# Two attention layers on one core: softmax shares turned by VectorE and spread by DMA, and the second pass in another order

## The chip, the core and the metric

The kernel runs on one core of one Trainium2 chip. A core has a matrix engine (TensorE, PE in the profile), a vector engine (VectorE, DVE), an activation engine (ScalarE, ACT), a general engine (GpSimd, POOL) and a queue engine (SyncE, SP) that issues most of the DMAs. Sixteen DMA engines move the data. On-chip data lie in SBUF (128 partitions); TensorE writes to PSUM, from which VectorE and ScalarE read. Each engine works through its own instructions strictly in order and waits on semaphores, so a late operand holds everything that is queued behind the waiting instruction on that engine.

The metric is the device time of one execution in microseconds (us). Before the change the median of four runs is 3569.33 us, from 3559.91 to 3572.44.

## What is computed

Two layers on 8 images of 32 x 32 places with 512 channels, all in fp32. The first is group norm, a projection to queries, keys and values, attention with 8 heads of 64 channels over all 1024 places, and an output projection that is added to the input:

```
qkv    = groupnorm(x) @ w_qkv + b_qkv
weight = softmax(q k^T / 64)              # 1024 x 1024 per head and image
x      = x + (weight @ v) @ w_out + b_out
```

The second is deformable attention. The first layer's result is layer-normed; a strided 7x7 depthwise convolution of its query projection gives 256 sampled places per image; keys and values come from these; then attention of all 1024 places over the 256 samples, an output projection and a small MLP:

```
att   = softmax(q k^T) @ v                # 1024 x 256 per head and image
z     = att @ mo_w + mo_b + x
out   = gelu(layernorm(z) @ mlp_w + mlp_b) + z
```

In both layers the softmax is split: scores minus their row maximum go through the exponential, whose row sums are gathered on the way, and the product with the values is divided by the sums only at the end. "Shares" are these reciprocals of the sums.

## The kernel before, in words

Work is cut in units. Each handles one pair of heads (two heads of 64 channels fill 128 partitions) and some query rows. The two passes keep one list of steps, `due`: `at(place, step)` (L348) files a step at a place counted in units, and `run_due` (L351) runs all steps below a place in order of place. An order wrapper (`InOrder`, L43) keeps each engine's instructions in the order of the program, so the places fix the order on every engine. What runs is: L387 to L799 the first pass, L802 to L1244 the second.

**First pass** (L387). A unit is 128 query rows of one image and one pair of heads against 1024 keys: 8 images x 4 pairs x 8 = 256 units. `MovedAttention.push` (L189) makes the scores (`scores`, L91: matmul into the PSUM tiles `sc`, row maxima `nmax` on VectorE, exponentials `e` with their sums on ScalarE), turns them in blocks of 32 x 32 on VectorE (`sq`), and after each second unit `moved` (L205) issues 16 DMAs that finish the transposition (`et<-sq`). Three units later `part` (L216) multiplies `et` with the values into `av`, of which PSUM holds one buffer. Four units make a block of 512 rows; at its end the shares are applied. In between, the `due` list holds the next projections, norms, the previous image's output projection, and depthwise convolution taps for the second layer.

**Second pass** (L802). A unit is 512 query rows and one pair of heads against 256 keys: 8 images x 2 halves x 4 pairs = 64 units. `unit_steps` (L1136) files, for unit n: scores at n, `moved` for each head at n + 0.12 and n + 0.14 (turn by VectorE, store to memory `sq_d<-sq`, load back `et<-sq_d`), shares at n + 0.2, their turn at n + 0.62, the product with the values at n + 1.15 and the scaling at n + 1.155; the next unit's query projection at n + 0.17. `back_steps` (L1060) files the output side, one tile of 128 rows per unit: `joined` (output projection `mm<-wo,attH`, sum `z` and its statistics) at n + 0.05, `norm` (`zn`) at n + 0.13, `turned` (transposition `mm<-ident,zn`, copies `zT`) at n + 0.6, `mlp` (`mm<-wm,zT`, the last projection) at n + 0.72, `biased` at n + 0.95, and for two tiles together `gelu` and `end`. `rstd` inside `joined` needs one small POOL instruction (`mv<-mv,minus_half`), for which `norm` waits. `conv_steps` (L1164) adds convolution taps in two lanes: lane 0 on VectorE (`chunk<-pad,dww,chunk`), lane 1 on ScalarE (`parts`) with the additions on POOL (`chunk<-parts,chunk`); `point_steps` (L1189) adds the sampling of the next image.

**The shares**, in both passes (L157 to L178). The sums lie with query rows on partitions, the product `av` has channels on partitions and query rows along the free dimension, so the shares must be turned. `share` takes the reciprocal on VectorE and copies each value 64 times (`rep`, 128x512); `turn` has TensorE transpose `rep` in four 128x128 pieces (`mm<-ident,rep`) and ScalarE copy the result to `inv`; `scale` multiplies `av` by `inv` on VectorE. This happens once in each block of the first pass (64) and once in each unit of the second (64).

## Time and profile before

| | |
|---|---|
| median of four runs | 3569.33 us |
| the profiled execution | 3555.69 us |
| its span on the core | 3554.0 us |
| PE busy | 3438.4 us (97%) |
| DVE busy | 2550.3 us (72%) |
| ACT busy | 1894.3 us (53%) |
| POOL busy | 1560.0 us (44%) |
| first pass | from the start to about 2220 us |
| preparation of the second pass | about 2220 to 2308 us |
| second pass, 64 units | 2308.71 us to the end |
| granted clock of TensorE | 0.992 in the mean |

The page gives busy time of each engine over the span. A share of busy time is an average over stages with different limits, so the windows (busy time of each engine in chosen stretches) are read beside it. The list of waits tells, for each engine, which other engine's result ended its idle time. The timeline lists instructions in order of time: start, duration, engine, operation, output <- inputs, shapes, count, and in brackets the idle time before it and what ended it. Matmuls are pipelined, so the starts of neighbours tell more than the durations. Almost all instructions carry line L54, that of the order wrapper; they are told apart by their tiles.

### The profile page before, as it was taken

How to read it: one execution, taken by the hardware profiler on the slowest of the kernel's cores; microseconds unless marked ns; L12 is line 12 of the kernel's file. 1: busy time of each engine (PE TensorE's matmuls, PEld its weight loads, DVE VectorE, ACT ScalarE, POOL GpSimd, SP SyncE). 2: the span in 40 equal slices, each digit the busy share in tenths (PEclk: the TensorE clock that was granted, in tenths of full speed). 3: DMA queues.
4: the chain of work that ended last, by engine and by line, in shares of the span. 5: the costliest groups of instructions: out<-in, count | busy, mean ns of one | idle time of the engine just before them, and what ended most of it. 6: DMA issues, size and time to landing. Idle time of an engine off the chain costs nothing.

```text
span 3554.0 us, 45846 instructions
## 1 busy us (share of the span) xinstructions
PE 3438.4 (97%) x15080; PEld 1712.3 (48%) x15080; DVE 2550.3 (72%) x3373; ACT 1894.3 (53%) x4061; POOL 1560.0 (44%) x1899
## 2 busy tenths in 40 slices
PE   7999999999999999999999998889999999999998
PEld 3554554554554554455455454534444444444443
DVE  4767778888888888888888786166778577564554
ACT  2443356576566566566567562245556465644442
POOL 1002226646646646655655654214445354531222
PEclk9999999999999999999999999999999999999999
DMA  4656666656656656666656667444545454454543
GB/s 141 162 152 170 181 160 188 195 148 177 206 157 176 197 158 174 193 165 184 192 166 163 190 169 206 126 153 159 195 156 188 148 183 167 162 204 159 189 142 118
DMA packets 358525, 606.01 MB, mean 171 GB/s; under 512 B 54576, under 2 KB 152880, under 8 KB 356240
## 3 DMA queue, kind: packets, MB, share of 16 engines
q1 hardware_dynamic: 327648, 500.99, 47.5%
q0 software_dynamic: 29488, 100.00, 9.1%
q8 instruction: 120, 1.97, 0.2%
q10 hardware_dynamic: 1152, 2.10, 0.2%
q14 instruction: 117, 0.96, 0.1%
HBM read 212.83 MB, written 121.63 MB: 94 GB/s over the span
## 4 chain that ended last, share of the span: by engine, by line
PE 82%; DVE 5%; ACT 4%; POOL 3%; DMA 3%; issue 2%; SPq 1%; ACTq 0%; POOLq 0%; DVEq 0%
PE mm L54 52%; PE sc L54 16%; PE av L54 14%; ACT e L54 2%; DVE sq L54 2%; SPq L54 1%; DMA et<-sq_d 1%; DVE nmax L54 1%; POOL chunk L54 1%; DMA et<-sq 1%; DMA sq_d<-sq 1%; DVE stats L54 1%; POOL res L54 0%; DVE zn L54 0%; ACT L54 0%
## 5 line engine op out<-in xcount | busy, mean ns | idle before, releaser
L54 ACT ACTIVATE e<-sc,nmax 128x1024 f32<-128x1024 f32 (+1 forms) x1024 | 802.8, 797 | 562.2 <-DVE nmax L54 561.5
L54 DVE TENSOR_REDUCE nmax<-sc 128x1 f32<-128x1024 f32 (+1 forms) x640 | 752.3, 1216 | 318.0 <-PE sc L54 317.6
L54 POOL TENSOR_TENSOR oa<-part_x,oa 128x256 f32<-128x256 f32 x852 | 646.1, 758 | 590.1 <-ACT part_x L54 544.4
L54 DVE STREAM_TRANSPOSE sq<-e 128x1024 f32<-128x1024 f32 x640 | 766.8, 1228 | 130.8 <-ACT e L54 111.1
L54 ACT ACTIVATE part_x<-pad_x,dww_x 128x256 f32<-128x256 f32 x852 | 437.0, 543 | 230.9 <-POOL oa L54 228.7
L54 PE MATMUL sc<-k,q 64*128 64x512 f32 x2048 | 535.3, 619 | 15.1 <-ACT e L54 13.2
L54 PE MATMUL av<-et,v 128*64 128x256 f32 x4096 | 501.1, 387 | 8.3 <-DMA et<-sq 7.6
L54 PE MATMUL mm<-xT,wqkv 128*128 128x512 f32 x1024 | 469.7, 603 | 3.1 <-issue 3.1
L54 PEld LDWEIGHTS av<-et,v 128*64 128x64 f32 x4096 | 274.0, 137 | 313.0 <-issue 161.9
L54 POOL TENSOR_TENSOR mv<-mv,minus_half 128x1 f32<-128x1 f32 x128 | 79.1, 618 | 698.7 <-DVE mv L54 692.1
L54 PEld LDWEIGHTS sc<-k,q 64*128 64x128 f32 x2048 | 185.9, 187 | 276.3 <-issue 195.5
L54 PEld LDWEIGHTS mm<-xT,wqkv 128*128 128x128 f32 x1024 | 187.4, 191 | 234.5 <-issue 228.9
L54 POOL TENSOR_TENSOR chunk<-parts,chunk 128x256 f32<-128x256 f32 x240 | 180.9, 754 | 188.9 <-ACT parts L54 174.6
L54 PEld LDWEIGHTS mm<-wqkv,xT 128*128 128x128 f32 x2048 | 234.2, 192 | 20.3 <-issue 18.9
L54 PE MATMUL mm<-wqkv,xT 128*128 128x128 f32 x2048 | 243.4, 277 | 0.0
L54 PE MATMUL mm<-wm,zT 128*128 128x512 f32 x512 | 235.6, 603 | 6.1 <-ACT zT L54 3.2
L54 PE MATMUL mm<-hat_h,wqq 128*128 128x512 f32 x512 | 237.7, 607 | 0.0
L54 PE MATMUL mm<-wo,attH 128*128 128x512 f32 x512 | 236.3, 604 | 0.0
L54 PE MATMUL mm<-w,attT 128*128 128x512 f32 x512 | 234.0, 602 | 0.0
L54 DVE SCALAR_TENSOR_TENSOR od<-pad_x,dww_x,od 128x256 f32<-128x256 f32 x276 | 219.5, 795 | 5.5
L54 ACT ACTIVATION_READ_ACCUMULATOR e<-sc,nmax 128x1 f32 x1024 | 209.2, 204 | 0.0
L54 DVE TENSOR_TENSOR res<-mm,bm_row 128x512 f32<-128x512 f32 x64 | 44.1, 690 | 213.2 <-PE mm L54 212.9
(165 smaller groups left out, 3907.2 us busy)
## 6 DMA issues: line engine op xcount, KB each, us to landing
et<-sq SPq DMA_DIRECT2D x2048, 128.0 KB, 2.7
sq_d<-sq SPq DMA_DIRECT2D x128, 512.0 KB, 4.7
et<-sq_d SPq DMA_DIRECT2D x128, 512.0 KB, 4.3
hat_h<-hat_d SPq DMA_DIRECT2D x16, 1024.0 KB, 6.9
xr<-mid SPq DMA_DIRECT2D x64, 256.0 KB, 4.5
x<-in_x_dram POOLq DMA_DIRECT2D x60, 256.0 KB, 3.9
out_dram<-res POOLq DMA_DIRECT2D x60, 256.0 KB, 4.4
w<-in_L_conv_w_out_dram POOLq DMA_DIRECT2D x14, 1024.0 KB, 7.8
```

Source lines behind the costliest of these rows:

```text
L54: return self.tc.keep_in_program_order(op(*args, **kwargs))
```

## The change

Shares. VectorE writes the 8 reciprocals of a row into one of two kept 128x32 tiles, whose other columns hold 1.0 from the start, and transposes this tile in its 32x32 blocks (`rsT`). SP stores the turned tile to memory (16 KB, `rs_d<-rsT`), and `spread` has SP load it back twice (`inv<-rs_d`), each load repeating one head's shares over 64 partitions. `turn`, with its TensorE transpositions and its ScalarE copy, is gone, and so is the copy `rep`. The sums are laid out by head first. `scale` reads and writes through a four-dimensional view. In the first pass the store is filed two units before the place of the old `share` and the loads one unit after the store; in the second pass both are filed directly with the unit's other moves, and there are two `inv` tiles.

Second pass. In a unit the first `moved`, the shares, the second `moved` and the loads of `inv` come at n + 0.02 to n + 0.041, ahead of the sums and statistics of `joined` (n + 0.05). The query projection comes at n + 0.06, the product at n + 1.1, so it now stands behind the output projection and the query projection. `mlp` and `biased` go from n + 0.72 and n + 0.95 to n + 1.03 and n + 1.035: the last projection of a tile stands behind the next unit's scores. `gelu` and `end` move by about one unit. The early four taps of lane 1 go from n + 0.156 to n + 0.045, ahead of `joined`. The last tiles before the end keep places of their own. `add_row`'s helper tile uses the pool of the rows `xr`.

```
-        rs = self.work.tile([P, NQT, 2], F32, tag="rs2", name="rs2", bufs=2)
-        nc.vector.reciprocal(rs, sums)
-        self.rep = self.work.tile([P, QB], F32, tag="rep", name="rep", bufs=1)
-        nc.vector.tensor_copy(
-            self.rep.rearrange("p (n d) -> p n d", d=HD),
-            rs.rearrange("p i h -> p (i h)").unsqueeze(2).to_broadcast([P, 2 * NQT, HD]),
-        )
-
-    def turn(self):
-
-        nc = self.nc
-        ps = self.ps_mm.tile([P, QB], F32, tag="mm", name="mm")
-        for i in range(NQT):
-            nc.tensor.transpose(ps[:, ts(i, P)], self.rep[:, ts(i, P)], self.ident)
-        self.inv = self.work.tile([P, QB], F32, tag="inv", name="inv", bufs=1)
-        nc.scalar.copy(self.inv, ps)
-
-    def scale(self, out):
-        self.nc.vector.tensor_tensor(out, self.av, self.inv, ALU.mult)
+        rs = self.shares[self.turns % 2]
+        self.turns += 1
+        nc.vector.reciprocal(rs[:, 0 : 2 * NQT], sums.rearrange("p h i -> p (h i)"))
+        turned = self.work.tile([P, SQ], F32, tag="rsT", name="rsT", bufs=2)
+        nc.vector.transpose(turned, rs)
+        self.share_d = self.dram.tile([P, SQ], F32, tag="rs_d", name="rs_d", bufs=3)
+        nc.sync.dma_start(self.share_d, turned)
+
+    def spread(self):
+
+        inv = self.work.tile([P, NSQ, NQT, SQ], F32, tag="inv", name="inv", bufs=self.n_inv)
+        there = self.share_d.rearrange("(r c) q -> r (c q)", r=NSQ)
+        for h in range(2):
+            self.nc.sync.dma_start(
+                inv[ds(h * HD, HD)].rearrange("p r i q -> p r (i q)"),
+                there[:, ts(h, NQT * SQ)].partition_broadcast(HD),
+            )
+        return inv
+
+    def scale(self, out, inv):
+        out, av = (t.rearrange("p (i r q) -> p r i q", i=NQT, q=SQ) for t in (out, self.av))
+        self.nc.vector.tensor_tensor(out, av, inv, ALU.mult)
...
-            at(n + 0.9, lambda: att.share(sums))
-            at(n + 1.04, att.turn)
+            at(n - 1.1, lambda: att.share(sums))
+            at(n - 0.1, lambda: share.update(inv=att.spread()))
             at(n + 1.85, scale)
...
-                over = n_units <= start + step * t and not tail
+                over, eve = (start + step * t >= n_units - i and not tail for i in range(2))
                 n, pair = start + step * t, start + step * (t - t % 2)
-                places = (pair - 1.6, pair - 0.5), (n + 0.05, n + 0.13), (n + 0.6, n + 0.72, n + (0.73 if over else 0.95))
+
+                ends = (n + 0.6, n + 1.03, n + 1.035)
+                if eve:
+                    ends = (n + 0.61, n + 0.72, n + 0.73) if over else (n + 1.06, n + 1.62, n + 1.625)
+                places = (pair - 1.6, pair - 0.5), (n + 0.05, n + 0.13), ends
...
-                    (gelu, 0.27 if tail else 0.735 if over else 0.96),
-                    (end, 0.28 if tail else 0.74 if over else 1.24),
+                    (gelu, 0.27 if tail else 0.735 if over else 1.72),
+                    (end, 0.28 if tail else 0.74 if over else 2.24),
...
-            at(n + 0.12, lambda: att.moved(u, 0))
-            at(n + 0.14, lambda: att.moved(u, 1))
-            at(n + 0.2, lambda: att.share(u["sums"]))
-            at(n + 0.62, att.turn)
+            at(n + 0.02, lambda: att.moved(u, 0))
+            at(n + 0.039, lambda: att.share(u["sums"]))
+            at(n + 0.04, lambda: att.moved(u, 1))
+            at(n + 0.041, lambda: u.update(inv=att.spread()))
             last = n + 1 == 2 * B * NHP
-            at(n + (1.3 if last else 1.15), lambda: att.product(u))
-            at(n + (1.305 if last else 1.155), scale)
+            at(n + (1.3 if last else 1.1), lambda: att.product(u))
+            at(n + (1.305 if last else 1.2), scale)
             if not last:
-                at(n + 0.17, lambda: query_step(*divmod(n + 1, NHP)))
+                at(n + 0.06, lambda: query_step(*divmod(n + 1, NHP)))
...
-                            place = 0.25 + 0.01 * j if not lane else 0.156 + 0.002 * j if j < 4 else 0.73 + 0.01 * j
+                            place = 0.25 + 0.01 * j if not lane else 0.045 + 0.001 * j if j < 4 else 0.65 + 0.01 * j
```

## Prediction

> **What bounds the kernel now.** I read the page's first part, then the windows of the two passes, then PE's waits, then timelines of single units.
>
> ```profile
> PE 3438.4 (97%) x15080; PEld 1712.3 (48%) x15080; DVE 2550.3 (72%) x3373; ACT 1894.3 (53%) x4061; POOL 1560.0 (44%) x1899
> ```
>
> ```profile
> 100.00:2130.00 2030.00, 2018.19 (x10018) 1030.29 (x10016) 1632.73 (x1964) 1179.92 (x2186) 1010.72 (x1260) 1.00 0.63 175
> 2130.00:2345.00 215.00, 186.82 (x747) 97.93 (x744) 90.63 (x143) 54.09 (x122) 59.30 (x65) 0.95 0.53 159
> 2345.00:3480.00 1135.00, 1095.39 (x3834) 516.40 (x3832) 740.02 (x1138) 610.28 (x1658) 460.86 (x531) 1.00 0.49 172
> ```
>
> The windows give length, busy time of PE, PEld, DVE, ACT and POOL, the granted clock, and the DMA share. In the first pass PE lacks 12 us of 2030, in the second 40 of 1135, with the clock at 1.00 in both. DVE is at 80% and 65%. So what PE no longer does is time saved, as long as its order brings no new waits. Its waits over the whole span:
>
> ```profile
> PE mm L54 <- DVE rep L54: 19.5, 23, 3.1
> PE av L54 <- DMA et<-sq_d: 18.2, 9, 4.1
> PE sc L54 <- ACT e L54: 13.2, 16, 1.8
> ```
>
> The first two lie nearly all in the second pass (3.1 of the 19.5 do not), the third in the first. One shares turn in the first pass, by the timeline:
>
> ```profile
> 1022.03 1.95 PE L54 MATMUL av<-et,v 128*64 128x256 f32 x16
> 1023.91 0.66 PE L54 MATMUL mm<-ident,rep 128*128 128x128 f32 x4
> 1024.40 3.60 PE L54 MATMUL mm<-xT,wqkv 128*128 128x512 f32 x8
> ```
>
> From start to start the four transpositions take 0.49 us. The reader should see that the 0.66 us of the row overlap the next matmuls. And one plain unit of the second pass:
>
> ```profile
> 3408.44 2.00 PE L54 MATMUL sc<-keys,q 64*128 64x256 f32 x16
> 3410.36 3.70 PE L54 MATMUL mm<-wo,attH 128*128 128x512 f32 x8
> 3414.00 1.94 PE L54 MATMUL av<-et,vals 128*64 128x512 f32 x8
> 3415.86 3.70 PE L54 MATMUL mm<-hat_h,wqq 128*128 128x512 f32 x8
> 3419.40 0.60 PE L54 MATMUL mm<-ident,zn 128*128 128x128 f32 x4
> 3420.45 0.66 PE L54 MATMUL mm<-ident,rep 128*128 128x128 f32 x4 [0.45 <-DVE rep L54]
> 3420.95 3.60 PE L54 MATMUL mm<-wm,zT 128*128 128x512 f32 x8
> ```
>
> The next scores start at 3424.48: a pitch of 16.04 us, of which transpositions and the wait for `rep` are 1.05 to 1.1.
>
> **The change, part by part.**
>
> *Turning the shares, first pass.* Removed from PE: 64 x 0.49 = 31.4 us, all on the path. ACT loses 64 copies of 0.59 us and DVE 64 copies `rep` of 0.43 to 0.9 us; PE waits 11.3 us for ACT's exponentials between 100 and 2220 us, in pieces of up to 1.8, and I give a fifth of it back (bounds 0 and 11). DVE gains a 128x32 transposition. None is shown alone; the reciprocal of 8 columns (0.18 us) and the 1024-column `sq` (1.23 us) bound it, and I take 0.2, nearer the small row. It stands where DVE has 20% free and costs nothing; without that cover it would cost 64 x 0.2 = 13 us. `scale` stays at 0.65 us: `pad`, also a strided view of a PSUM row of 512, takes 0.69 beside 0.69 for the plain `z`.
>
> *The DMAs of the first pass.* SP gets three more issues per block, past its 32 `et` DMAs:
>
> ```profile
> 1010.77 10.38 SPq L54 DMA_DIRECT2D et<-sq  x16
> ```
>
> Sixteen issues take 10.4 of the 16.5 us of two units, so three more at 0.3 to 0.6 us fit. The store waits for DVE's `rsT`, the loads for the store's landing; behind them stand the next pair's `et`. The store follows the preceding pair's issues, and the loads come 16 issues later, when it has long landed. The loads go out about 10.4 to 11 us after that pair's `sq`; the scaling follows the next pair's `sq`, 16.5 us after the first, and the next `av`, which needs the one PSUM buffer back, must start 3 us later. So a load may take 8 us after its issue before PE stops (about 5.5 before DVE does). Landing times shown:
>
> ```profile
> et<-sq SPq DMA_DIRECT2D x2048, 128.0 KB, 2.7
> bq_x<-in_L_conv_bq_dram POOLq DMA_DIRECT2D x1, 256.0 KB, 3.7
> bo_row<-in_L_conv_mo_b_dram SPq DMA_DIRECT2D x1, 256.0 KB, 11.3
> ```
>
> The last two are rows repeated over 128 partitions; 11.3 us was measured among loads of 1 MB. I take 3.7, nearest in kind and in load: cost nothing. At 11.3 PE would lose 3.3 us in each block, 211 us in all. The added 82,000 packets, at queue 1's mean (47.5% of 16 x 3554 us for 327,648, so 82 ns), add at most 0.12 to the DMA share of 0.63.
>
> *End of the first pass.* There PE waits 3.07 us for `rep` (2202.08). SP's `et` issues end at 2192.8; a store landing in 2.2 us (the 2 KB load `bv_c`) to 4.7 (`sq_d`), two issues of 0.6 and 3.7 us put `inv` at 2199.9 to 2202.4 and the scaling 3.5 to 1 us earlier than its end at 2204.1. I take -3, nearest the small row (bounds -5 and +3, as those issues can run late).
>
> *Second pass, what leaves PE.* The order of a plain unit becomes scores 1.93, `mlp` 3.53, `joined` 3.53, query 3.63, product 1.87, `zn` 0.44: 14.93 us by the starts above, against 16.04. The copies `zT` (0.65 us) used to lie under the transpositions of `rep`; now the scores cover them.
>
> *The product's wait.* `et` lands about 21 us after its scores' start (3429.9 against 3408.44: issue at 3425.58 plus 4.3 landing). It was needed at the pitch plus 5.6 = 21.6 us, so every delay was paid: 18.2 us. Now it is needed at 14.9 + 12.6 = 27.5. The store of the shares sits on SP between the two heads' moves (+0.4), `inv` after both, needed only by `scale`, 2 us after the product. The waits go, except some microseconds in the first units, which have no output side to cover them.
>
> *What is late next: `zn`.* VectorE now does `sq`, `res`, the shares and `sq` before `z`. In a unit without convolution: maxima from 2.0 to 4.4 us after the scores' start, exponentials to 7.0, first `sq` to 6.5, `res` 7.1, shares 7.5, second `sq` 8.8, `z` and statistics 10.9, POOL's power 11.6, `zn` 12.7. PE wants it at 14.5: covered by 1.8 us. With lane 1 active the cover is gone. Its four additions (0.75 us each) now stand before the power on POOL, and its last three taps and the two `gelu` with two table loads (1.28 each) delay the next exponentials from 3.3 to about 6.6 us. Then `zn` comes at 15.4 and PE waits about 1 us. In the unit after the sampled rows are gathered, POOL's gathers (about 1.25 us each, four) delay the third tap, that the exponentials and all that follows: about 4.8 us. Behind the waiting `zn` on PE stand the next scores.
>
> Summed over units 7 to 41, starts 2429.35 to 3115.41, 686.1 us: with PE's instructions alone, by the rows' durations, 648 us. New waits: eleven plain units, four of them gather units at 4.8, the others at about 1, and 2 for the rest: 28 (bounds 0 and 60; the upper end is 4.8 us in all eleven plus 7). Net -10. Units 42 to 62, 373.3 us, have no taps: 349, net -24. Units 0 to 6, 120.6 us, come to about 102 by the same sums with a 20.5 us latency for `et`: -18. At the end one last projection more lies behind the final product, against 2 us of waits that go: +2.
>
> Sum: first pass -31 - 2 - 3 = -36; second -10 - 24 - 18 + 2 = -50. Together -86 against the profiled execution (span 3554.0, time 3555.69). The median of the runs shown is 13.6 us above that execution, so I take the difference from the median: 3569 - 86, about **3484 us**.
>
> **Two rules of the Trainium skill beside the rows.** "TensorE: Matmul & The Clock Gate", Part 4: PE-mode transpose, gives about 275 ns for a 128x128 transposition in a kernel. The duration row (284 ns) agrees, but 0.49 us for four shows how they overlap; priced at 275 ns, the 512 would be worth 141 us instead of 63, and the forecast would be about 3406. "DMA: Bandwidth & Descriptors", Measured (HBM to SBUF), speaks against the change: transfers under 64 KB are dominated by descriptors. Its section on the anatomy of a DMA puts the fixed part at about 2 us; by that, an estimate of 2.0 for the store and 2.3 for a load lies within the slack and changes nothing in the sum.
>
> **Rivals.**
> *A: the loads come late, and it is slower.* A first-pass load that lands L us after issue costs 64 x (L - 8). With -86 otherwise, the change is lost from L = 9.4. For it: 11.3 us in a row of this profile, and the DMA engines at 0.63. Against: 3.7 us in a first-pass row, and `et` landing at 2.7 amid that same load. At 10 us the time would be 3484 + 128 = 3612.
> *B: the second pass becomes a ring of VectorE, ScalarE and POOL.* If the waits for `zn` reach the upper bound of 60 and the first units gain nothing, 3484 + 32 + 18 = 3534. For it: VectorE's loop from maxima to maxima is some 14.9 us with five taps of 0.84, PE's pitch 14.9. Against: nothing stands in the way from unit 42 on.
> *C: no new waits.* `zn` is always in time, and ACT's waits go too: 3484 - 28 - 9 = 3447. For it: taps take 0.51 us where POOL is quiet. Against: POOL's order, which is fixed.
> *D: the change does not do what it says.* The transpositions filled gaps, so their 63 us do not come back, nor the 18 of the first units: 3484 + 63 + 18 = 3565. Against it is the 0.49 us between starts, with no idle time on either side.
>
> **How the numbers follow.** Main case 0.58, C 0.17, B 0.15, A 0.07, D 0.03. The main case's own range, from half to one and a half times the new waits and the bounds at the end of the first pass, is 3468 to 3502. To leave no more than 0.2 out, the range reaches past C nearly to its end and takes in B: 3450 to 3536. A time within 0.3% (11 us) can't be told from no change here. Main, B and C are faster: 0.90. A gives slower 0.07; D, close to no change, is split into 0.02 same and 0.01 slower.
>
> **What would show it.** PE should have no `mm<-ident,rep`; units of the second pass from 42 on should follow each other at 14.9 to 15.0 us; the wait of `av` for `et<-sq_d` should be under 5 us; a wait of PE for `zn` of 15 to 45 us should appear in the units with taps; `inv<-rs_d` should land in 2.5 to 5 us, with no wait of `attT` for it; the window from 100 to 2130 should lose its blocks' 0.49 us. It is wrong if DVE waits for DMA before scaling, if SP falls behind with `et`, or if the plain pitch stays at 16.

## The result, and the profile after

The changed kernel takes 3565.80 us (median of 39 runs, 3557.69 to 3576.80) against 3563.86 us before (63 runs, 3556.12 to 3573.74): a ratio of 1.0005, with an interval of 1.000 to 1.001. Within what can be measured the change is worth nothing; 3484 us was forecast, worked out from a median of before that was 5 us higher. The profiled execution has a span of 3562.8 us, 8.8 more than that of before. From here on "gain" and "loss" are differences of profiled executions against that of before, unless a ratio is given. There is one profiled execution of each kernel, so a difference of a few us in one stage is not sure by itself: in the eleven experiments below that have word for word the same first pass, it came to -11.5 to -17.1 us against before, and the stretch behind it to +3.7 to +10.6.

The first part of the page (busy time of each engine) and the windows of the three stages, in the columns of the table shown for before:

```profile
PE 3406.4 (96%) x14568; PEld 1686.4 (47%) x14568; DVE 2526.8 (71%) x3373; ACT 1809.0 (51%) x3919; POOL 1539.5 (43%) x1903
```

```profile
100.00:2130.00 2030.00, 1994.55 (x9717) 1006.83 (x9718) 1594.04 (x1956) 1142.05 (x2112) 993.71 (x1252) 0.99 0.66 182
2130.00:2345.00 215.00, 185.47 (x702) 96.52 (x700) 85.94 (x133) 54.45 (x114) 65.01 (x75) 0.88 0.52 153
2345.00:3480.00 1135.00, 1080.61 (x3648) 512.95 (x3650) 757.52 (x1151) 559.86 (x1585) 448.15 (x527) 0.97 0.58 188
```

PE does 512 fewer instructions and is busy 32 us less, but its idle time in the first window has gone from 12 to 35 us, and in the last from 40 to 54. The granted clock fell as well, to 0.99, 0.88 and 0.97, where it had been 1.00, 0.95 and 1.00. PE's and VectorE's waits over the whole span (us in total, times, longest) say for what:

```profile
PE mm L54 <- DVE zn L54: 42.0, 17, 4.9
PE av L54 <- DVE attT L54: 18.8, 7, 3.7
PE av L54 <- DMA et<-sq: 17.6, 3, 8.1
PE sc L54 <- ACT e L54: 17.0, 17, 2.0
PE av L54 <- DMA et<-sq_d: 8.4, 3, 4.2
```

```profile
DVE attT L54 <- DMA inv<-rs_d: 62.5, 34, 7.2
```

The waits for `rep` are gone and those for `et<-sq_d` are down from 18.2 us, as was meant. New are 18.8 us for `attT`, the scaled product of the first pass, which on VectorE waited for its shares to arrive. Waits for `zn` are 42.0 us.

Since every unit starts with its scores, the differences of these starts show where the time lies:

| stretch | forecast | after minus before |
|---|---|---|
| first pass, to its last scores | -33 | +17.3 |
| from there to the second pass | -3 | +11.5 |
| second pass, units 0 to 6 | -18 | -10.1 |
| units 7 to 41 | -10 | +9.9 |
| units 42 to 62 | -24 | -23.9 |
| from the last unit's start to the end | +2 | +4.1 |

In the first pass each block gains 0.39 us, 25 us in all. Most of the loss stands in one place of each image but the first, unit 28 of its 32: +5.0, +2.3, +6.7, +4.3, +3.6, +5.9 and +5.0, together 33 us. (Another 4 us stand in units 7 and 8, the other 5 in pieces below 1 us.) In the first six of these seven places PE waited for `attT`, 2.26 to 3.70 us; in the last, unit 252, it waited 4.78 us for `et<-sq`. The third of the seven, in the timelines of SP, VectorE and PE:

```profile
1046.20 2.36 DVE L54 STREAM_TRANSPOSE sq<-e 128x1024 f32<-128x1024 f32 x2
...
1048.62 11.01 SPq L54 DMA_DIRECT2D et<-sq  x16
...
1058.80 2.37 DVE L54 STREAM_TRANSPOSE sq<-e 128x1024 f32<-128x1024 f32 x2 [1.23 <-ACT e L54]
1059.68 1.28 SPq L54 DMA_DIRECT2D inv<-rs_d  x2
1060.76 1.99 PE L54 MATMUL sc<-k,q 64*128 64x512 f32 x8
...
1065.70 0.69 DVE L54 TENSOR_TENSOR attT<-av,inv 128x512 f32<-128x512 f32 x1 [4.53 <-DMA inv<-rs_d]
1066.45 3.68 PE L54 MATMUL av<-et,v 128*64 128x256 f32 x16 [3.70 <-DVE attT L54]
1070.06 4.87 PE L54 MATMUL mm<-xT,wqkv 128*128 128x512 f32 x8
```

The loads of `inv` stand behind 16 issues of `et` that fill SP until 1059.68. VectorE finished the next pair's `sq` at 1061.17 and had nothing in front of the scaling but the load, which came 4.53 us later. PE could not start the next `av` for want of the one PSUM buffer. The reader should also see what the wait did to PE: the 16 products behind it took 3.61 us from start to start, where they take 1.88, and the next group 4.80, where it takes 3.63. The wait was 3.70 us, the unit lost 6.67.

The plain unit of the second pass came out as forecast (14.88 us from scores to scores, for 14.93; 16.04 before):

```profile
3419.03 2.00 PE L54 MATMUL sc<-keys,q 64*128 64x256 f32 x16
3420.96 3.70 PE L54 MATMUL mm<-wm,zT 128*128 128x512 f32 x8
3424.50 3.60 PE L54 MATMUL mm<-wo,attH 128*128 128x512 f32 x8
3427.93 3.60 PE L54 MATMUL mm<-hat_h,wqq 128*128 128x512 f32 x8
3431.46 1.94 PE L54 MATMUL av<-et,vals 128*64 128x512 f32 x8
3433.33 0.66 PE L54 MATMUL mm<-ident,zn 128*128 128x128 f32 x4
3433.91 2.00 PE L54 MATMUL sc<-keys,q 64*128 64x256 f32 x16
```

But around the sampling of the next image units lost time: 14 (+4.2), 21 (+4.4), 22 (+2.2), 29 (+4.3), 30 (+2.8), 37 (+4.3) and 38 (+2.5), each with a wait for `zn`.

### The profile page after: what moved, and what is told of

Read it like the earlier page. It is cut to its first block, busy times and chain, and to the rows that moved or that the text cites. A ratio compares the mean times of both kernels' runs of the same rounds, so it can differ in the third digit from the quotient of the medians.

```text
span 3562.8 us, 45200 instructions
## 1 busy us (share of the span) xinstructions
PE 3406.4 (96%) x14568; PEld 1686.4 (47%) x14568; DVE 2526.8 (71%) x3373; ACT 1809.0 (51%) x3919; POOL 1539.5 (43%) x1903
## 4 chain that ended last, share of the span: by engine, by line
PE 75%; DVE 6%; SPq 5%; ACT 4%; POOL 4%; DMA 4%; issue 3%; POOLq 0%; DVEq 0%; ACTq 0%
PE mm L54 48%; PE sc L54 14%; PE av L54 13%; SPq L54 5%; ACT e L54 2%; DMA inv<-rs_d 2%; POOL chunk L54 1%; DVE sq L54 1%; DVE chunk L54 1%; POOL oa L54 1%; ACT L54 1%; DVE nmax L54 1%; DMA et<-sq 1%; POOL row L54 0%; DVE smp L54 0%
## 5 line engine op out<-in xcount | busy, mean ns | idle before, releaser
L54 POOL TENSOR_TENSOR oa<-part_x,oa 128x256 f32<-128x256 f32 x852 | 636.4, 747 | 594.0 <-ACT part_x L54 549.0
L54 PE MATMUL av<-et,v 128*64 128x256 f32 x4096 | 510.6, 393 | 37.4 <-DVE attT L54 18.8
L54 PE MATMUL mm<-w,hat_x 128*128 128x512 f32 x384 | 172.7, 600 | 0.0
```

The lines of the kernel that those rows point to most:

```text
L54: return self.tc.keep_in_program_order(op(*args, **kwargs))
```

## The experiments

All of them, with the ratio to the kernel before that was run beside each. All but the second have the early loads, and those from the ninth to the thirteenth the late gathers too:

| run | time, us | ratio (interval) |
|---|---|---|
| early loads | 3531.47 | 0.9909 (0.9893 to 0.9924) |
| first pass of the change only | 3597.58 | 1.0096 (1.0082 to 1.0109) |
| second pass: shares only | 3554.44 | 0.9973 (0.9960 to 0.9986) |
| second pass: order only | 3562.38 | 0.9998 (0.9989 to 1.0006) |
| late gathers | 3513.03 | 0.9843 (0.9817 to 0.9869) |
| taps away | 3528.64 | 0.9886 (0.9861 to 0.9911) |
| late gathers, taps away | 3508.97 | 0.9836 (0.9815 to 0.9857) |
| sum first | 3526.85 | 0.9890 (0.9865 to 0.9915) |
| POOL apart | 3518.48 | 0.9882 (0.9864 to 0.9899) |
| end by POOL | 3515.60 | 0.9873 (0.9853 to 0.9893) |
| POOL apart, end by POOL | 3526.33 | 0.9887 (0.9868 to 0.9906) |
| POOL apart in some units, end by POOL | 3514.45 | 0.9852 (0.9835 to 0.9869) |
| POOL apart in some units, `xr` earlier | 3499.52 | 0.9817 (0.9796 to 0.9838) |
| shares only, product as cover | 3523.56 | 0.9889 (0.9869 to 0.9908) |
| TensorE's turn, product as cover | 3569.24 | 1.0016 (1.0004 to 1.0027) |

**Early loads: the place of two DMAs in SP's queue.**

```
-            at(n - 0.1, lambda: share.update(inv=att.spread()))
+            at(n - 0.3, lambda: share.update(inv=att.spread()))
```

> The changed kernel with one place moved: in the first pass the two loads of the shares (inv<-rs_d) are filed 0.2 units earlier, so that SP issues them ahead of the next pair's 16 et DMAs (10.4 to 11.0 us of issue in the trace of the changed kernel) and not behind them. Theory 1 (the loads come late, because they queue behind those issues; the waits of attT for inv and the lower clock after them cost the first pass its gain): the wait of attT for inv (62.5 us in 34 pieces) falls below 10 us, the +2.3 to +6.7 us at unit 28 of seven images (33 us) and most of the +11.5 us at the end of the first pass go, the last scores of the first pass start at about 2145 (2166.3 before, 2183.6 in the changed kernel), and the whole comes to 3515 to 3535. Theory 2 (the first pass lost its gain because the shorter units make VectorE late with group norm and sq, whatever the loads do): the time stays at 3560 to 3572 and unit 28 still loses 2 us or more.

Measured: 3531.47 us, inside Theory 1's range. VectorE's waits for `inv` in the first pass fell from 62.5 us to this, and in the same unit of the same image SP, VectorE and PE now show:

```profile
DVE attT L54 <- DMA inv<-rs_d: 2.3, 1, 2.3
```

```profile
1031.23 0.33 SPq L54 DMA_DIRECT2D rs_d<-rsT  x1
1032.67 1.26 SPq L54 DMA_DIRECT2D inv<-rs_d  x2
1037.58 11.02 SPq L54 DMA_DIRECT2D et<-sq  x16
...
1049.72 1.99 PE L54 MATMUL sc<-k,q 64*128 64x512 f32 x8
1050.05 0.65 DVE L54 TENSOR_TENSOR attT<-av,inv 128x512 f32<-128x512 f32 x1
...
1051.63 1.95 PE L54 MATMUL av<-et,v 128*64 128x256 f32 x16
```

The loads now go out 17 us ahead of the scores of unit 28, not 1.1, and unit 28 of images 1 to 6 loses nothing (0.0 in the mean). The last scores of the first pass start at 2150.39 (Theory 1 said about 2145). Theory 2 is out. What did not go is +5.3 us at unit 252, in the last image, where PE still waits for `et<-sq` (5.12 us), and +6.6 us up to the second pass.

**The first pass alone.** The second pass is given the old `share`, `turn` and `scale` in a class of its own, and all its places are those of before.

```
-        att = Attention(nc, ident, ps_mm, ps_sc, ps_av, work, dram, 2)
+        att = TurnedAttention(nc, ident, ps_mm, ps_sc, ps_av, work, dram, 2)
```

> The first pass of the changed kernel, with the second pass as before (turn by TensorE, order of before). Theory 1: the first pass alone is slower, by 17 us to its last scores and 29 us to the first scores of the second pass; the second pass is as before, so 3585 to 3600. Theory 3 (the first pass is as good as before on most executions and the loss lies in the second pass): 3545 to 3566.

Measured: 3597.58 us, 0.96% slower than before. The first pass by itself was worse than what it replaced, +20.1 us to its last scores, and the second pass hid that. From there to the second pass it lost 3.8 us, where the changed kernel with the same first pass had lost 11.5. Theory 3 is out.

**The two halves of the second pass.** "Shares only" keeps the DMAs and puts back all places of before, with the shares just ahead of the second head's move (first lines); "order only" keeps the new places and puts back the turn by TensorE (last two):

```
-            at(n + 0.039, lambda: att.share(u["sums"]))
+            at(n + 0.139, lambda: att.share(u["sums"]))
...
-            at(n + 0.041, lambda: u.update(inv=att.spread()))
+            at(n + 0.62, lambda: u.update(inv=att.turn()))
```

> Early loads in the first pass as in the run with the moved place; in the second pass the shares go by VectorE and DMA, but the steps keep the order of before (mlp ahead of the next scores, shares just ahead of the second head's move). Theory 1: the first pass gains about 21 us; in the second pass the transpositions of rep (0.5 us a unit) and the waits for rep (16 us) go, but et still lands about 21 us after its scores while the product wants it 5.6 us after the next scores, so the pitch of plain units only falls from 16.04 to about 15.5 to 15.7 and waits for et<-sq_d grow to 20 to 35 us; second pass -10 to -30, whole 3512 to 3535. No waits for zn above 15 us. Rival: the new order is what costs, and without it the second pass reaches 14.9 us a unit: whole below 3500.

> Early loads in the first pass; in the second pass the new order, but the shares turned by TensorE as before (rep on VectorE, four transpositions at n + 0.62). Theory 1 (the waits for zn in the units that sample, 14, 21, 22, 29, 30, 37 and 38, come from the order: taps, corners and gathers now lie ahead of what zn needs): they stay, 35 to 60 us, and each plain unit carries 0.45 to 0.55 us more than with the shares by DMA, so the time is 22 to 35 us above the run with early loads alone. Rival (the loads of inv on SP and the store make them): the waits for zn fall below 20 us and the time is within 10 us of that run.

Measured, in units 42 to 62, which have no taps: shares only +3.3 us, order only -14.6, both (with early loads) -22.6. Shares only, at 3554 us, misses both forecasts: the pitch of plain units falls only to 15.80 us at best, and units 44, 46 and 51 lose 4.4 us together. Its timeline shows why there is so little to gain:

```profile
3416.27 3.70 PE L54 MATMUL mm<-hat_h,wqq 128*128 128x512 f32 x8
3419.81 0.60 PE L54 MATMUL mm<-ident,zn 128*128 128x128 f32 x4
3421.01 3.70 PE L54 MATMUL mm<-wm,zT 128*128 128x512 f32 x8 [0.60 <-ACT zT L54]
```

`mlp` needs the copies `zT` that ScalarE makes of the transposed `zn`. Before, the transpositions of `rep` ran in that gap; without them PE waits for the copies (37.3 us in 61 pieces). Order only came out in time as Theory 1 said, 31 us above early loads alone; the plain pitch is 15.32 us, 0.44 more. Waits for `zn` are 34.6 us (35 to 60 was said), so the sampling units' waits come with the order, not with the shares' DMAs. It also has waits that early loads alone do not have: 13.5 us for `co` in units 13, 21, 29 and 37, and 5.4 for `pad`.

**Late gathers, taps away, both, and the sum first.** Four suspects for the waits for `zn`: POOL's row gathers ahead of lane 1's additions, three lane 0 taps ahead of the row maxima, both, or the second `sq` ahead of `z`.

```
-            for h, (p0, p1) in enumerate(((0.8, 1.22), (1.23, 2.22))):
+            for h, (p0, p1) in enumerate(((0.8, 1.22), (1.7, 2.22))):
...
-                        count = 7 if lane else 3 if points else 5
+                        count = 7 if lane else 0 if unit % (2 * NHP) == NHP else 3 if points else 5
...
-                places = (pair - 1.6, pair - 0.5), (n + 0.05, n + 0.13), ends
+                places = (pair - 1.6, pair - 0.5), (n + 0.036, n + 0.13), ends
```

> The run with early loads (3531 us), with one more place moved: in the second pass the four row gathers for the second half of the samples are filed behind the late additions of lane 1 on POOL (place 1.7 and not 1.23 after the sampling unit); the orders of PE, VectorE, ScalarE and SP are the same. Theory 1b (in units 14, 22, 30 and 38 zn is late because the gathers, waiting on POOL for the sampled rows, hold lane 1's additions, these a tap on ScalarE, that the gelu and the exponentials): these four units and those after them lose their +2 to +4 us against before, units 21, 29 and 37 keep +4.3, and the time falls by 12 to 22 us, to 3509 to 3520. Rival (VectorE's order, with the second sq ahead of z, makes zn late everywhere): no change, 3527 to 3535.

> The run with early loads (3531 us), and in the second pass no taps of lane 0 in the units 12, 20, 28 and 36 (three in each before; they move one unit on). Theory 1a (in units 21, 29 and 37 zn is late because three taps, slowed to 5.7 us beside POOL's work, and the sampling's small steps stand ahead of the row maxima on VectorE): units 21, 29 and 37 fall from +4.3 to -0.5 or less against before, units 22, 30 and 38 keep a part, and the time falls by 10 to 18 us, to 3513 to 3521. Rival (order of sq and z): no change, 3527 to 3535.

> Both moves together, gathers behind lane 1's additions and no lane 0 taps in the sampling unit. Theory 1a with 1b: the gains add, units 7 to 41 come to -20 to -28 us against before (+10.6 with early loads alone), waits for zn fall from 43 to below 12 us, and the time is 3493 to 3505. Rival (another cause takes the place of each, POOL's load as a whole): 3510 or more.

> The run with early loads (3531 us), with the sum z and its statistics filed ahead of the shares and the second sq on VectorE (place n + 0.036); PE's order is the same. Rival theory (VectorE's new order of sq and z makes zn late): zn comes 1.6 us earlier in each unit, waits for zn fall from 43 to below 20 us, units 7 to 41 gain 15 us or more, time 3505 to 3517. Theory 1 (the maxima or the exponentials are late in a few units by 4 us and more): only 1.6 us in each of eleven units, less what et then comes late, time 3515 to 3530.

Measured: late gathers 3513.03 us, a hit. Against early loads alone units 22 and 30 go from +2.3 and +3.0 to -2.2 and -2.5, units 14 and 38 only from +3.9 and +2.1 to +1.7 and +0.1, units 21, 29 and 37 keep +4.0 to +4.4, and units 7 to 41 go from +10.6 to -9.7. The chain in unit 22 of the changed kernel (scores at 2740.43), in the timelines of POOL and ScalarE:

```profile
2740.60 1.38 POOL L54 DMA_INDIRECT row<-mid,ii  x1 [1.85 <-DVE smp L54]
...
2746.20 2.35 POOL L54 TENSOR_TENSOR chunk<-parts,chunk 128x256 f32<-128x256 f32 x3
...
2746.98 0.55 ACT L54 ACTIVATE parts<-pad,dww 128x256 f32<-128x256 f32 x1 [4.95 <-POOL chunk L54]
...
2751.30 0.47 ACT L54 ACTIVATE e<-sc,nmax 128x256 f32<-128x256 f32 x1
```

and in the same unit with late gathers (scores at 2702.86):

```profile
2704.18 1.86 POOL L54 TENSOR_TENSOR chunk<-parts,chunk 128x256 f32<-128x256 f32 x2 [3.00 <-ACT parts L54]
2704.94 0.56 ACT L54 ACTIVATE parts<-pad,dww 128x256 f32<-128x256 f32 x1 [0.49 <-POOL chunk L54]
...
2706.20 0.99 POOL L54 DMA_INDIRECT row<-mid,ii  x1 [0.16 <-issue]
...
2709.26 0.47 ACT L54 ACTIVATE e<-sc,nmax 128x256 f32<-128x256 f32 x1
```

The first exponential starts 6.4 us after the scores and not 10.9. Taps away (3528.64 us) falls: units 21, 29 and 37 stay at +3.4 to +3.5. The sum of the two is a miss as well (3508.97 us, above 3505). The sum first gives 3526.85 us, with 32.5 us of waits for `zn`, as Theory 1 had it: the new order of `sq` and `z` is not what makes `zn` late by 4 us. The taps' failure shows in VectorE's timeline. With the three taps in place (first fence, the changed kernel), they take 5.71 us; without them (second fence, late gathers with taps away) the small steps that follow take the time instead, 8.5 us from the first `co` to `nmax`, where the changed kernel takes 3.8:

```profile
2720.04 5.71 DVE L54 SCALAR_TENSOR_TENSOR chunk<-pad,dww,chunk 128x256 f32<-128x256 f32 x3
2725.67 0.15 DVE L54 TENSOR_TENSOR co<-mm,refs 128x4 f32<-128x4 f32 x1
...
2729.52 2.35 DVE L54 TENSOR_REDUCE nmax<-sc 128x4 f32<-128x1024 f32 x2
```

```profile
2684.51 0.14 DVE L54 TENSOR_TENSOR co<-mm,refs 128x4 f32<-128x4 f32 x1
...
2693.06 2.35 DVE L54 TENSOR_REDUCE nmax<-sc 128x4 f32<-128x1024 f32 x2
```

In both kernels POOL works through its output sums, additions of `bo_row` and lane 1's additions beside them.

**POOL apart, the end by POOL, and all.** The output sums go from n + 2.24 to n + 1.74, the additions of `bo_row` with their loads from pair - 0.5 and pair - 1.6 to pair - 1.2 and pair - 2.2. In the second run the shares' DMAs of the last three blocks of the first pass are issued by POOL.

```
-                places = (pair - 1.6, pair - 0.5), (n + 0.05, n + 0.13), ends
+                places = (pair - 2.2, pair - 1.2), (n + 0.05, n + 0.13), ends
...
-                    (end, 0.28 if tail else 0.74 if over else 2.24),
+                    (end, 0.28 if tail else 0.74 if over else 1.74),
...
-        nc.sync.dma_start(self.share_d, turned)
+        self.queue.dma_start(self.share_d, turned)
```

> The run with early loads and late gathers (3513 us), with POOL's output sums (end) and additions of bo_row filed half a unit to a unit earlier, into the stretch where POOL was idle, so that POOL no longer works from 2 us before the scores of units 21, 29 and 37 to 7 us after them; the orders of PE, VectorE and ScalarE are the same. In the run without taps in the sampling unit the sampling's 25 small steps on VectorE took 8.5 us beside that work, against 3.8 us in the trace of the changed kernel, where the three taps took it instead (5.7 us). Theory 1c (VectorE's taps and small steps are slowed by POOL's elementwise work beside them, whichever stands there): taps and small steps together fall from 9.5 us to 6 us or less, units 21, 29 and 37 fall from +4.3 to 0 or less, whole 3495 to 3505. Rival (the number of steps ahead of the maxima is what counts): units 21, 29 and 37 stay at +3.5 to +4.4, whole 3508 to 3517.

> The run with early loads and late gathers (3513 us), with the stores and loads of the shares of the last three blocks of the first pass issued by POOL, which is idle there, and not by SP. Theory (in the last image's short units SP's issues are the limit: 16 et issues take 10.4 us of some 10.3 us of PE's pair, and each block's store, the wait for its landing and the two loads cost SP about 4 us more): the +5.2 us at unit 252 and most of the +6.6 to 8.4 us from the last scores to the second pass go, waits of av for et<-sq fall from 11 to 14 us to under 8, whole 3500 to 3507. Rival (those waits come from et's landing itself, or from fewer cover on PE): no change, 3509 to 3517.

> Early loads, late gathers, POOL's sums apart from the sampling, and the last blocks' shares on POOL's queue, together. If the causes are separate the gains add: 3484 to 3498. If one of the last two theories falls, 3497 to 3508.

Measured: POOL apart does what Theory 1c says at its place. The taps and the small steps take 5.9 us instead of 9.5, and units 21, 29 and 37 go to +0.2 to +0.3:

```profile
2675.28 1.52 DVE L54 SCALAR_TENSOR_TENSOR chunk<-pad,dww,chunk 128x256 f32<-128x256 f32 x3
2676.72 0.15 DVE L54 TENSOR_TENSOR co<-mm,refs 128x4 f32<-128x4 f32 x1
...
2681.14 2.35 DVE L54 TENSOR_REDUCE nmax<-sc 128x4 f32<-128x1024 f32 x2
...
2711.40 0.55 DVE L54 TENSOR_SCALAR zn<-z,mv 128x512 f32<-128x512 f32 x1 [5.85 <-POOL mv L54]
```

The last line is where the time went: in the gather units POOL's moved sums now stand ahead of the power that `zn` needs, units 14, 22, 30 and 38 lose 2.7 to 4.8 us, and the whole is 3518.48, a miss. The end by POOL (3515.60, a miss) takes the +4.9 us of unit 252 away (-0.5), and PE then waits 12.8 us for the last block's `attT`, whose loads stand behind POOL's own late steps. All together is worse than late gathers alone.

**POOL apart in some units only.** The moves of POOL's steps are kept only for the steps that fell into the unit that begins the sampling; the last block's shares go by SP.

```
+                crowded = [(u % (2 * NHP)) == NHP for u in (pair - 1, n + 2)]
+                places = (pair - 1.6, pair - (1.2 if crowded[0] else 0.5)), (n + 0.05, n + 0.13), ends
...
+                    (end, 0.28 if tail else 0.74 if over else 1.74 if crowded[1] else 2.24),
```

> Early loads and late gathers (3513 us), POOL's output sums and additions of bo_row moved half a unit to a unit earlier only where they fell into the unit that begins the sampling (4, 12, 20, 28, 36, 44 and 52) and not in the gather units, where they stood ahead of the power that zn waits for (5.9 us on VectorE in the run with all of them moved); and only the blocks of units 247 and 251 have their shares' DMAs on POOL, the last block's go by SP again (behind POOL's work they made PE wait 12.8 us). Theory 1c with the SP theory: units 21, 29 and 37 at +0.3 against before, units 22, 30 and 38 at -2 as with late gathers, the last scores of the first pass at about 2147 and the second pass 146 us later, whole 3488 to 3499. Rival (POOL is full, and each of its steps only moves the wait): 3505 or more.

Measured: 3514.45 us, a miss with a cause of its own. The loads of `xr` had kept their place, so the additions waited for them, and the power behind, as in unit 60:

```profile
3410.40 2.49 POOL L54 TENSOR_TENSOR xr<-xr,bo_row 128x512 f32<-128x512 f32 x2 [5.41 <-DMA xr<-mid]
3412.85 0.56 POOL L54 TENSOR_TENSOR mv<-mv,minus_half 128x1 f32<-128x1 f32 x1
```

At the end of the first pass the loss at unit 252 went (-0.7), but +11.5 us then stood between the last scores and the second pass, where early loads had +5.3 and +6.6. These 11.5 us lie 0.9 above the spread named at the start, so they are no sure loss. That the three added issues are the limit behind unit 252 is not shown: PE's wait for `et<-sq` behind the last scores is 6.47 us with early loads and 7.32 where POOL issues the shares.

**Two questions that were left.** With the `xr` loads moved too, and all blocks' shares by SP:

```
+                places = (pair - (2.2 if crowded[0] else 1.6), pair - (1.2 if crowded[0] else 0.5)), (n + 0.05, n + 0.13), ends
```

> Early loads, late gathers, and POOL's sums and additions moved out of the units that begin the sampling, with the loads of xr now 0.6 units earlier too: in the run before, the additions waited 5.4 us on POOL for xr (in unit 60, for example), and the power for zn behind them. Blocks of the first pass by SP alone. Theory 1c: units 20, 21, 28, 29, 36 and 37 fall to -1.5 and +0.3 as in the run with all of POOL's sums moved, units 22, 30 and 38 stay at -2, units 42 to 62 at -20 or better, whole 3496 to 3506. Rival (POOL is full, every step only moves the wait): 3509 or more.

Measured: 3499.52 us, a hit. Units 7 to 41 come to -24.0, units 21, 29 and 37 to +0.3, +0.2 and +0.5; unit 38 keeps +0.9. This is the fastest version: 1.8% below the kernel before, with an interval of 1.6 to 2.0%.

The other question was whether TensorE's transpositions in the second pass are a saving only when other work fills their gap. The order of before is kept, and the product moves into the gap:

```
-            at(n + (1.3 if last else 1.15), lambda: att.product(u))
-            at(n + (1.305 if last else 1.155), scale)
+            at(n + (1.3 if last else 1.65), lambda: att.product(u))
+            at(n + (1.305 if last else 1.7), scale)
```

> Shares alone in the second pass gave nothing (units 42 to 62 at +3.3 us against before), while shares and new order gave -23. In its place between zn's transpositions and mlp PE now waits 0.60 us for ScalarE's copies zT, which rep's transpositions had covered. Here the order of before stays, shares go by DMA, and only the product (and its scaling) moves, to between zn's transpositions and mlp (n + 1.65), so that it covers the copies and et has 4 us more to land. Theory 5 (rep's transpositions stood in a gap that the copies zT leave; with other work there they are a saving): no waits for zT, pitch of plain units 14.9 to 15.0, and no sampling units with +4 us, since zn, gelu and lane 1 keep their places of before: units 7 to 41 at -25 to -35 us, 42 to 62 at -20 to -24, whole 3485 to 3505. Rival (the order of before has another limit, VectorE's or et's loop of 21 us): pitch 15.4 or more, whole 3520 or more.

> The same place of the product (n + 1.65), but in the second pass the shares are turned by TensorE as before (rep's transpositions behind the product). Theory 5: with the product as cover, rep's transpositions cost their 0.45 to 0.55 us a unit, so this is 25 to 36 us slower than the run with the shares by DMA in the same order: 3512 to 3540. Rival (they stay in a gap): within 8 us of it.

Measured: with the shares by DMA 3523.56 us. The waits for `zT` are 2.1 us and no sampling unit loses 4 us, but the plain pitch is 15.23 to 16.05, since `zn` now comes up to 0.9 us late behind the first `sq`, and units 12, 20, 28 and 36 each wait 2.95 us for `th`, a step of the sampling (0.46 with early loads). With TensorE's turn in the same order 3569.24 us, 46 more, of which 10 lie in units 42 to 62 (0.48 us a unit, and 0.38 to 0.39 in units 47 to 49, which wait for nothing in either). In units 7 to 41 it is 41, more than the transpositions alone can be: units 7, 15, 23, 31 and 39 wait up to 2.9 us for `q` (11.4 us in all), and the waits for `th` grow from 11.8 to 17.2 us; those for `zn` hardly differ there (8.8 and 9.5). So Theory 5 holds for what the transpositions are worth in units 42 to 62: with the product as cover the shares by DMA are 10.1 us faster than TensorE's turn (-18.7 against -8.6), without it they were 3.3 slower. Both times lie above its ranges, and the rival's mark (3520 us or more, another limit in the order of before) is met too.

## Why the prediction was wrong, step by step

*The DMAs of the first pass: the step that failed.* "So a load may take 8 us after its issue before PE stops (about 5.5 before DVE does)" was worked out from 16.5 us, the median distance of two units. At unit 28 the next pair's `sq` ended 12.6 us after the last (1048.56 to 1061.17), since the one before had been late behind group norm's small steps and the units there are short. Minus 11.0 us of issues, 1.5 us were left to VectorE, not 5.5, and the scaling could start only 6.0 us after the first load's issue. The trace of before had this distance in the same place, 1046.38 to 1059.00 (VectorE's timeline of before):

```profile
1044.02 2.36 DVE L54 STREAM_TRANSPOSE sq<-e 128x1024 f32<-128x1024 f32 x2
...
1056.63 2.37 DVE L54 STREAM_TRANSPOSE sq<-e 128x1024 f32<-128x1024 f32 x2 [1.23 <-ACT e L54]
```

The landing itself was sized fairly: 3.7 us assumed, 3.9 in the median of the first pass (3.3 to 5.3). That was in part luck, since the row it was taken from, `bq_x`, was issued at 25.9 us, ahead of the first `et` (53.9 us), and so not amid the load of the first pass. The estimates beside the sum, 2.0 us for the store and 2.3 for a load, were too low: 3.7 and 4.4 in the median of all. VectorE waited in 34 of the 64 blocks, PE for `attT` in 7, six of them at unit 28. Rival A had the mechanism (the loads come late) and the wrong form: not a loss in every block from 9.4 us of landing on, but one place in each image, with landings of 5.3 us at most. Moving the two loads ahead of the 16 issues gave 34 us back by the medians, which shows it. With this step alone put right the time is 3531 us, inside the range of 3450 to 3536, but still 47 above the forecast; the rest lies in the terms below.

*Turning the shares, first pass.* 0.49 us a block was the distance of two starts; removing it gave 0.39, because the group behind takes 0.1 us more (for the 32 matmuls `mm<-wqkv,xT`, 3.77 us from start to start, and 3.67 behind the transpositions). This is a mis-sized term of 6 us. ScalarE's waits, for which 2 us were to come back, rose from 13.2 to 17.0 (15.6 with early loads).

*End of the first pass.* -3 was forecast, +11.5 came; with early loads +6.6, and +3.8 in the run with the first pass of the change only, so the size is not sure. The forecast followed only the last block's shares. Where nothing fills the units, SP's issues (10.4 us for a pair, and the store, its landing and the two loads on top) stand against a pair of short units. Taken off SP, they no longer cost unit 252 its 5 us, which shows that much; the wait for `et<-sq` behind the last scores stayed, so the cause of the rest is open.

*Second pass, what leaves PE.* The pitch (14.88 for 14.93) and units 42 to 62 (-23.9 for -24) are right. Right too is the reason given, "The copies `zT` (0.65 us) used to lie under the transpositions of `rep`; now the scores cover them": shares without that order gave +3.3. Rival D, that the transpositions filled gaps, was wrong for the first pass and right for the second in the old order. Its price of 3565 us is the time that came, but by luck: the transpositions did come back in the first pass (25 us) and in units 42 to 62, and other waits took it away again. The product's wait went as said, but for 3.3 us in unit 4 and the last unit.

*What is late next.* That `zn` would be late, and through POOL's gathers, lane 1's tap and the gelu, was right, and late gathers show it. Two sizes were right as well: the gather units 14, 22, 30 and 38 waited 3.9 to 4.9 us for 4.8, and units 12, 20, 28 and 36 waited 0.9 for about 1. The other sizes were not. Units without a wait gained 0.75 us in units 7 to 41, 26 in all 35 and not 38: where before had no wait for `rep`, 0.73 came back, and only the plain units gave 1.1. Eleven units lost 36 us against that, and not 28. VectorE's steps beside POOL's, which the sum did not have, made units 21, 29 and 37 wait 4.5 us each instead of about 1 (POOL apart shows it), and behind the waits of 3.5 us and more PE's granted clock was 0.71 to 0.83 for 10 us, where it was 1.00 behind those of 1.3 and less. Units 0 to 6 came to -10 for -18 (units 4 and 5 wait 3.3 us for `et<-sq_d`, 2.5 for `q` and 3.5 for `zn`), and the end to +4 for +2. The second pass as a whole gave -20 us for -50, between the main case and rival B, which has it at 0. (The last step of the sum is out by one: 3569 minus 86 is 3483, not 3484.)

*What would show it.* Of the marks that were named, the pitch, the absence of `mm<-ident,rep`, a `zn` wait inside 15 to 45 us and `inv` landing at 2.5 to 5 us in the median were met. The wait for `et<-sq_d` was 8.4 us and not under 5, a block of the first pass lost 0.39 us and not 0.49 while the pass as a whole got longer, and "with no wait of `attT` for it" failed: "DVE waits for DMA before scaling" was the first of the three conditions named for an error.

## What to carry to other kernels

The slack of a load is the smallest distance in the loop, not the middle one, and it is counted from its own issue: look in the trace of before for the shortest pair of units and for what the queue has in front. Two loads that need one thing long finished belong ahead of sixteen issues that do not wait for them; here 0.2 units of place were worth 0.9%. Before an instruction's time is taken as a saving, look whether the instruction behind it has another operand that comes no earlier; and when one engine's queue order is changed, follow POOL's single small instruction that everything waits for.

## What the runs showed of the hardware

*A short wait can cost more than its length, and its length does not say whether.* At unit 28 of four images, by PE's timeline and the windows of 10 us around it: a wait of 2.26 us lost 2.33 and one of 3.53 lost 3.60, with a granted clock of 1.00; one of 2.63 lost 4.34 and one of 3.39 lost 4.99, with 0.83. The windows of these four, in the order of the program (waits of 3.39, 2.26, 2.63 and 3.53 us):

```profile
508.00:518.00 10.00, 6.61 (x28) 2.94 (x25) 5.63 (x7) 4.29 (x9) 2.28 (x4) 0.83 0.81 228
785.00:795.00 10.00, 7.74 (x36) 3.35 (x34) 6.73 (x8) 5.11 (x10) 3.38 (x5) 1.00 0.83 233
1340.00:1350.00 10.00, 7.37 (x33) 3.47 (x32) 6.37 (x8) 4.93 (x10) 2.93 (x5) 0.83 0.77 222
1618.00:1628.00 10.00, 6.47 (x31) 3.00 (x31) 5.46 (x8) 4.02 (x9) 2.60 (x4) 1.00 0.78 227
```

The Trainium skill ("TensorE: Matmul & The Clock Gate", What's actually happening) describes a free-running window of about 3.4 us and half rate after an idle one. That the products behind the wait of 3.70 us took 3.61 us for 1.88 agrees with half rate, and that the length alone does not decide agrees with a window that runs freely; that a wait of 2.63 us went with a lower clock does not fit the rule of a whole idle window, as far as the profile's times go.

*VectorE beside POOL.* A tap of 128x256 took 0.5 us with POOL idle and 1.9 us beside POOL's additions, and the sampling's small steps 8.5 us beside a full stretch of POOL's work and 3.8 us where that ended early in them, while sums that read PSUM (`z`, 0.65 us) were the same in both. The Trainium skill ("SBUF — State Buffer", Who interferes with whom) says that a VectorE instruction with two inputs in SBUF contends with a GpSimd instruction that reads SBUF, and calls this contention over the shared ports an exclusive lock; the taps, with both inputs in SBUF, agree.
